# A routed three-layer network in fp32: another bank for layer 3 of odd tiles, and four steps that change places

## The chip, the cores and the metric

The kernel runs on one core of a Trainium2 chip. The metric is the device time of one execution in microseconds (us). Before the change it is 521.77 us, the median of three runs (521.76 to 522.54). All times below are microseconds from the start of the profiled execution's span, unless they are called ns.

## The reference

There are 4096 tokens of 256 numbers and 8 experts. Each expert is a network of three layers (256 to 512, 512 to 512, 512 to 256). A gate picks two experts for each token.

```python
gate = xn @ wg_W + wg_b + (genre_embed @ gg_W + gg_b)     # xn: x, RMS-normalised
gate_w = softmax(gate)
topk_w, topk_i = top_k(gate_w, 2)
cw = sum(one_hot(topk_i, E) * topk_w[..., None], axis=-2)
h1 = relu(einsum('bsh,ehm->bsem', x, W1) + b1)
h2 = relu(einsum('bsem,emn->bsen', h1, W2) + b2)
out_e = einsum('bsen,enh->bseh', h2, W3) + b3
return x + einsum('bseh,bse->bsh', out_e, cw)
```

## The kernel before

The kernel does not run every expert on every token. It computes the gate for all tokens, sorts the (token, expert) pairs by expert, and works through tiles of 128 pairs that belong to one expert. A tile's rows of x are gathered by an indirect DMA, and its results are added to the rows of the output by another. For these inputs there are 67 tiles.

**Banks.** PSUM's eight banks are the tiles PB[0] to PB[7]. Layers 1 and 2 of a tile use PB[0] to PB[3]: layer 1 the first 256 columns of each, layer 2 the others. PB[4] takes transposes of x. PB[5] takes layer 3: its first 256 columns for even tiles, its last 256 for odd ones (L780 to L784). PB[6] takes small things: column totals of the gate's counts in columns 448 to 463 (`totals`, L319 and L320), and the result of one transpose of the gate's values. PB[7] takes the gate's values, and later the index table.

**The front (0 to 29).** x is loaded, transposed on TensorE and multiplied with the gate's weights. The gate of a first part of the tokens (8 of 32 rows per partition, "A") is finished at once, which gives each expert its first tile: tile u of expert u, for u from 0 to 7. Near its end (L473 to L478) come two dummy transposes, `transpose_x(0)` (two transposes on TensorE, and a copy of the result, xT, by ScalarE), and `upright` (a copy of the gate's values from PB[7] to gTs by ScalarE, L218, four small transposes on TensorE, L221, into PB[6]), then a copy of that to graw.

**The head (steps 0 to 6, `head_step`).** Step u works on the first tile of expert u. Meanwhile the routing of all other tokens ("B") goes on, mostly on VectorE. It is a generator, `rest()`, that yields estimates of cost in ns; `more(3200)` draws from it until 3200 are spent or it yields None. Each step calls `more` twice. The seven first calls and the seven second calls draw the same steps wherever they stand. The second call of step 1 holds the totals (TensorE) and some twenty small VectorE operations behind them. Step 2 goes on to the first comparison (L577) of chunk 0 of 4 of the index table. The first call of step 3 holds the rest of chunk 0 (L579, L584) and begins chunk 1, and so on; `table()` issues the table's matmuls (L486) for whatever chunks have been issued. The first call of step 5 holds the gathers of x for tiles 8 to 11, and the second one some POOL operations and the write of the table cwdR.

Every engine executes its own instructions in the order in which this code issues them (`manual_schedule`), and the waits between engines follow from the data. In step u the order of issue is: gather x of tile u+3 (POOL); layer 1 of tile u (TensorE, with its activations on ScalarE, L765); first `more`; transpose of x of tile u+1; layer 3 of tile u-1 (L783); `table()`; layer 2 of tile u (L773, with its activations, L776); second `more`; then for tile u-1 `scaled` (bc = bias times weight, on ScalarE, L749) and `give` (y = layer 3 times weight plus bc, on VectorE, L792, and the scatter-add of y, POOL, L793); last the gather of tile u's weight columns, cg (`gather_cw`, POOL, from the DRAM table cwdA, L645). Tile 0's cg is gathered at the start of step 1. From step 3 on a copy of part of x into the output (SyncE, L842) follows; by the code's dependencies it stands behind the scatters before it.

**The rest (steps 7 and later, `step`).** Steps 8 to 31 work on pairs of tiles of one expert, later steps on single tiles. There x is transposed through DRAM (SyncE: L673 out, L679 back; VectorE: L687), the weights of the step's expert are copied by VectorE (L723, L728, L732, stages 1 to 3), and `scaled` runs on VectorE (L747). The order is: gathers, layer 1 with stage 2, cg of the next step, `scaled` of the step before, stage 1 and xT of the next step, layer 3 and `give` of the step before, stage 3, layer 2.

**The switch.** How many tiles there are is known only at run time. The count is loaded into a register of every engine at step 37, a hint of the branch is given at step 38, and behind step 38 every engine branches to the code for that count (`tc.Switch`), which begins with step 39.

Of the kernel before, what the change touches and what calls it, by code (L numbers as in the profile page):

```python
# [13 lines left out]
ALU = mybir.AluOpType  # L14
# [7 lines left out]
def kernel(  # L22
# [17 lines left out]
    nc = tc.nc  # L40
    V = nc.vector
# [138 lines left out]
    def squares(i, eng):  # L180
        xi = xin[i // TPB][:, i % TPB, :]
        if eng == "A":
            nc.scalar.activation(sqs[eng], xi, AF.Square, accum_out=ss[:, i : i + 1])
        else:
            V.tensor_tensor_reduce(sqs[eng], xi, xi, 1.0, 0.0, ALU.mult, ALU.add, ss[:, i : i + 1])
# [28 lines left out]
    def upright(nq, bank=PB[3], dst=PB[4], copied=False):  # L214

        R = 32 * nq
        if not copied:
            nc.scalar.copy(gTs[0:R, :], bank[0:R, :])  # L218
        gtp = dst[:, 0 : TPB * R].rearrange("p (k r) -> p k r", k=TPB)
        for k in range(TPB):  # L220
            nc.tensor.transpose(gtp[:, k], gTs[0:R, ts(k, P)], ident[0:R, 0:R])  # L221
        return gtp.rearrange("p k (q e) -> p q k e", q=nq)[:, :, :, 0:E]
# [229 lines left out]
    def second_part(some):  # L452

        j0 = GA + 4
        nc.scalar.copy(gTs, PB[3])
        for q in range(2):
            turn_pe(j0 + q, 0, q)
        raw = upright(4, copied=True)
        vps = PB[6][:, 384 : 384 + 2 * E * MC]
        nc.tensor.transpose(vps, vecs, ident[: 2 * E * MC, : 2 * E * MC])  # L460
        for i in range(NA + 10, NI - 4):
            if i == NI - 8:
                V.tensor_copy(vT.rearrange("p l e c -> p (l e c)"), vps)
            squares(i, "V")
        for q in range(2):
            turn_copy(q, "A")
        nc.scalar.copy(graw[:, NA : NA + 4 * TPB, :].rearrange("p (q k) e -> p q k e", q=4), raw)
        for q in range(2):
            turn(j0 + q, 1, 2 + q, "A")
        some(3)  # L470
        for c in range(HC):
            gates(c, (2 * c, 2 * c + 1), PB[7])
        busy(2)  # L473
        for i in range(NI - 4, NI):
            squares(i, "V")
        transpose_x(0)
        raw = upright(2, PB[7], PB[6])
        nc.scalar.copy(graw[:, j0 * TPB : NI, :].rearrange("p (q k) e -> p q k e", q=2), raw)  # L478

    mms = []  # L480
# [181 lines left out]
    def gather_cw(u):  # L662
        for b in tiles(u):
            cg = cgs[b] = ring(run, [P, E], "cg", 6, b)
            fetch(cg, (cwdA if b < E else cwdR)[:, :], b)
# [18 lines left out]
    def transpose_x(u):  # L684
        if u > E:
            for b in tiles(u):
                V.transpose(  # L687
                    xT[:, :, b % 2, :].rearrange("p c (k b) -> p k c b", b=SQ),
                    shs[:, b % 2].rearrange("p k (a c) -> p k c a", a=SQ),
                )  # L690
            return
        bs = tiles(u)
        w = len(bs)
        tp = PB[4][:, 0 : HC * w * BT].rearrange("p (c s t) -> p c s t", c=HC, s=w)
        for k, b in enumerate(bs):
            g = rows(b).rearrange("p (r c) -> p c r", c=HC)
            for c in range(HC):
                nc.tensor.transpose(tp[:, c, k, :], g[:, c], ident)
        nc.scalar.copy(xT[:, :, bs[0] % 2 : bs[0] % 2 + w, :], tp)
# [67 lines left out]
    def layer2(u):  # L767
        _, bb, w2 = ww[u][0:3]
        w = len(tiles(u))
        for n in range(MC):  # L770
# [4 lines left out]
                )  # L775
            nc.scalar.activation(hids[:, 1, n, 0 : w * BT], ph, AF.Relu, bias=bb[:, 1, n : n + 1])  # L776

    def layer3(u):
        w3 = ww[u][3]
        for k, b in enumerate(tiles(u)):  # L780
            po = PB[5][:, ts(b % 2, H)]
            for n in range(MC):
                nc.tensor.matmul(  # L783
                    po, lhsT=hids[:, 1, n, ts(k, BT)], rhs=w3[:, n, :], start=(n == 0), stop=(n == MC - 1)  # L784
                )

    def give(u):

        cws = ww.pop(u)[4]
        for b, (cw, bc) in zip(tiles(u), cws):  # L790
            y = ring(run, [P, H], "y", 2, b)
            V.scalar_tensor_tensor(y, PB[5][:, ts(b % 2, H)], cw, bc, ALU.mult, ALU.add)  # L792
            add = nc.gpsimd.indirect_dma_start(  # L793
                out=orows,
                out_offset=bass.IndirectOffsetOnAxis(ap=index(b), axis=0),
                in_=y,
                in_offset=None,
                bounds_check=NT - 1,
                oob_is_err=False,
                compute_op=ALU.add,  # L800
            )
            if b < E:
                for f in fills[1:]:
                    tc.declare_no_dep(add.ins, f.ins, reason="the first E tiles hold tokens of the first part alone")

            behind = [adds[-1]] if adds else [fills[0]]
            if b == E:
                behind += fills[1:]
            for a in behind:
                tc.add_manual_dep(  # L810
                    add.ins,
                    a.ins.name,
                    mybir.DependencyInfo(mybir.DependencyClass.Sync, mybir.DependencyReason.DATA),
                    reason="a token's row is read and written back",
                )
            adds.append(add)
# [3 lines left out]
    def head_step(u, more):  # L820

        if u + 3 < E:
            gather(u + 3)
        if u == 1:
            gather_cw(0)
        layer1(u)
        more(3200)
        transpose_x(u + 1)
        stage_1(u + 1)
        if u >= 1:  # L830
            layer3(u - 1)
        table()
        layer2(u)
        more(3200)
        if u >= 1:
            scaled(u - 1, "A")
            give(u - 1)
            gather_cw(u)

        if u >= E - 1 - NF:  # L840
            i = NA + (u - (E - 1 - NF)) * (NB // NF)
            fills.append(nc.sync.dma_start(our[:, i : i + NB // NF, :], xr[:, i : i + NB // NF, :]))  # L842
# [8 lines left out]
    def step(u, last, open_end=False):  # L851

        for v in ahead(u, last + 2 * open_end):
            for b in tiles(v):
                gather(b)
        far = E < u + 2 < last + open_end
        if far:
            stow(u + 2)
        if u < last:
            layer1(u)  # L860
            stage_2(u)
        if u + 1 < last:
            gather_cw(u + 1)
        scaled(u - 1)
        if u + 1 < last:
            stage_1(u + 1)
            if u + 1 > E:
                transpose_x(u + 1)
        if far:
            shuffle(u + 2)  # L870
        layer3(u - 1)
        give(u - 1)
        if u + 1 == E:
            transpose_x(u + 1)
        if u < last:
            stage_3(u)
            layer2(u)
# [18 lines left out]
    with tc.manual_schedule():  # L896
        some = first_part()
        for b in range(3):
            gather(b)
        second_part(some)  # L900
        other = rest()

        def routing(ns):
            while ns > 0:
                c = next(other, None)
                if c is None:
                    break
                ns -= c

        routing(100)  # L910
        stage_1(0)
        for u in range(E - 1):
            head_step(u, routing)
        for _ in other:
            pass
        gather_cw(E - 1)
        for u in range(E - 1, CUT):
            if u == CUT - 2:
                _, (nextra,) = nc.values_load_multi_w_load_instructions(
                    nex[0:1, 0:1],  # L920
                    min_val=0,
                    max_val=NREST - NSURE,
                    skip_runtime_bounds_check_because="the tiles behind the first E are NSURE to NREST",
                )
            elif u == CUT - 1:
                tc.switch_hint({e: nextra for e in ENGS}, NREST - NSURE + 1, "tail")
            step(u, SURE, True)
    kept = (ww, ex, cgs)
    state = [{k: list(v) if isinstance(v, list) else v for k, v in d.items()} for d in kept]
    done = list(adds)  # L930
    for k in tc.Switch(nextra, NREST - NSURE + 1, hint="tail"):
        for d, old in zip(kept, state):
            d.clear()
            d.update({b: list(v) if isinstance(v, list) else v for b, v in old.items()})
        adds[:] = done
        with tc.manual_schedule():
            for u in range(CUT, SURE + k + 1):
                step(u, SURE + k)


# [29 lines left out]
```

## Time and profile before

| | |
|---|---|
| median of 3 runs | 521.77 us |
| the profiled execution's own time | 521.67 us |
| its span in the profile | 519.9 us |
| granted TensorE clock, mean | 0.992 |
| instructions | 8677 |
| DMA traffic | 59.25 MB, 114 GB/s in the mean |
| step of a pair (steps 8 to 31), start to start of layer 1 | 13.8 us |
| step of a single tile, start to start of layer 1 | 7.1 us |

The span is what the profile covers; the execution's own time is 1.8 us longer. Engines: PE is TensorE's matmul, PEld its weight load, DVE is VectorE, ACT ScalarE, POOL GpSimd, SP SyncE. A row of the timeline gives start, duration, engine, line, operation, what it writes from what, how many were merged, and in brackets how long the engine was idle before and which work ended that. Ends of matmuls are modelled, so losses are better read from start to start. DMA bandwidth is full from the start to about 58 us: 23 MB are moved between 20 and 100 us, most of it the experts' weights.

### The profile page before, as it was taken

The numbers are of one execution on the slowest core, as the hardware profiler recorded it, in microseconds if no ns is written. First come the engines' busy times: TensorE is split into PE (matmuls) and PEld (weight loads), VectorE is DVE, ScalarE is ACT, GpSimd is POOL, SyncE is SP. The second block draws the span as 40 slices with busy tenths as digits, with TensorE's granted clock in tenths as the row PEclk, the third lists the DMA queues.
The fourth block names the chain that finished last, engine by engine and source line by source line (L and its number), as shares of the span: only waits on it lengthen the run. The fifth ranks groups of instructions, "written<-read, shape, count | busy, mean of one in ns | idle before, by whom it ended". The sixth has DMA issues, their size and how long they took to land. (4 is left out here: it accounts for less than half of the span.)

```text
span 519.9 us, 8677 instructions
## 1 busy us (share of the span) xinstructions
PE 500.8 (96%) x2848; PEld 447.1 (86%) x2848; DVE 226.1 (43%) x549; ACT 169.1 (33%) x415; POOL 286.7 (55%) x241
## 2 busy tenths in 40 slices
PE   8999898999999999999999999999999999999992
PEld 6678898888888888888888888888888889999891
DVE  4776872243443333333344343334433335655450
ACT  4763434222222222222222222222222223443340
POOL 5233466866555556545666655565555455765521
PEclk9999999999999999999999999999999999999996
DMA  8999954743433334334343343333334233433201
GB/s 265 389 412 401 381 133 133 177 106 72 81 69 71 80 67 85 73 82 83 78 83 73 74 80 78 77 79 71 73 71 81 43 82 57 96 68 68 40 4 22
DMA packets 68656, 59.25 MB, mean 114 GB/s; under 512 B 39905, under 2 KB 59570, under 8 KB 68340
## 3 DMA queue, kind: packets, MB, share of 16 engines
q1 hardware_dynamic: 52752, 41.21, 24.5%
q0 software_dynamic: 15136, 17.32, 20.6%
q8 instruction: 24, 0.39, 0.3%
q14 instruction: 36, 0.29, 0.2%
q10 hardware_dynamic: 708, 0.03, 0.1%
HBM read 42.80 MB, written 20.71 MB: 122 GB/s over the span
## 5 line engine op out<-in xcount | busy, mean ns | idle before, releaser
L773 PE MATMUL pb<-hid,big 128*128 128x256 f32 (+1 forms) x1120 | 211.0, 346 | 0.8 <-ACT hid L765 0.8
L773 PEld LDWEIGHTS pb<-hid,big 128*128 128x128 f32 x1120 | 187.0, 191 | 21.6 <-ACT hid L765 1.2
L793 POOL DMA_INDIRECT out_dram<-y,idxR x59 | 100.1, 1697 | 134.5 <-issue 57.5
L776 ACT ACTIVATE hid<-pb,bb 128x256 f32<-128x256 f32 (+1 forms) x140 | 61.7, 441 | 243.8 <-PE pb L773 231.5
L728 DVE COPY big<-w2a 128x2048 f32 x35 | 44.2, 1263 | 151.5 <-PE pb L773 151.5
L762 PE MATMUL pb<-xT,big 128*128 128x256 f32 (+1 forms) x560 | 108.3, 346 | 0.5 <-DVE big L723 0.5
L783 PE MATMUL pb<-big,hid 128*128 128x256 f32 x472 | 107.6, 379 | 0.0
L762 PEld LDWEIGHTS pb<-xT,big 128*128 128x128 f32 x560 | 93.5, 191 | 10.5 <-issue 0.6
L783 PEld LDWEIGHTS pb<-big,hid 128*128 128x128 f32 x472 | 88.8, 190 | 11.6
L645 POOL DMA_INDIRECT big<-in_x_dram,idxR x59 | 76.6, 1298 | 20.6 <-issue 11.9
L645 POOL DMA_INDIRECT cg<-cwdR,idxR x59 | 65.9, 1117 | 18.1 <-issue 18.1
L765 ACT ACTIVATE hid<-pb,bb 128x256 f32<-128x256 f32 (+1 forms) x140 | 60.9, 441 | 43.2 <-PE pb L762 33.4
L792 DVE SCALAR_TENSOR_TENSOR y<-pb,cw,bc 128x256 f32<-128x256 f32 x59 | 26.4, 480 | 59.2 <-PE pb L783 46.7
L723 DVE COPY big<-w1a 128x1024 f32 x35 | 24.3, 695 | 22.4 <-PE pb L762 18.2
L773 PE MATMUL pb<-hid,w2a 128*128 128x128 f32 x256 | 30.3, 276 | 0.1
L773 PEld LDWEIGHTS pb<-hid,w2a 128*128 128x128 f32 x256 | 29.7, 192 | 0.5 <-ACT hid L765 0.3
L793 POOL DMA_INDIRECT out_dram<-y,idxA x8 | 14.6, 1820 | 23.1 <-DVE y L792 22.5
L687 DVE STREAM_TRANSPOSE xT<-gTs 128x256 f32<-128x256 f32 x57 | 22.5, 425 | 5.0 <-DMA gTs<-scr 5.0
L732 DVE COPY big<-w3a 128x1024 f32 x35 | 24.2, 692 | 0.0
L747 DVE TENSOR_SCALAR bc<-b_sb,cw 128x256 f32 x59 | 23.2, 393 | 2.1
L776 ACT ACTIVATE hid<-pb,vT 128x128 f32<-128x128 f32 x32 | 11.8, 368 | 31.0 <-PE pb L773 29.3
L783 PE MATMUL pb<-w3a,hid 128*128 128x256 f32 x64 | 15.4, 384 | 3.3 <-DVE y L792 3.3
(204 smaller groups left out, 251.4 us busy)
## 6 DMA issues: line engine op xcount, KB each, us to landing
w2a<-in_L_cond_W_dram SPq DMA_DIRECT2D x8, 1024.0 KB
scr<-big SPq DMA_DIRECT2D x57, 128.0 KB
gTs<-scr SPq DMA_DIRECT2D x228, 32.0 KB
big<-in_x_dram SPq DMA_DIRECT2D x8, 512.0 KB
w1a<-in_L_cond_W_dram SPq DMA_DIRECT2D x8, 512.0 KB
w3a<-in_L_cond_W_dram SPq DMA_DIRECT2D x8, 512.0 KB
out_dram<-in_x_dram SPq DMA_DIRECT2D x4, 768.0 KB
out_dram<-in_x_dram SPq DMA_DIRECT2D x1, 1024.0 KB
```

The source lines that it names most:

```text
L645: nc.gpsimd.indirect_dma_start(out=dst, out_offset=None, in_=src, in_offset=bass.IndirectOffsetOnAxis(ap=index(b), axis=0), bounds_check=N ...
L723: V.tensor_copy(st1, w1a[:, e].rearrange("p e c m -> p (e c) m"))
L728: V.tensor_copy(st2, w2a[:, ex[u]].rearrange("p e c m -> p (e c) m"))
L732: V.tensor_copy(st3, w3a[:, ex[u]].rearrange("p e c m -> p (e c) m"))
L747: V.tensor_scalar(bc, b3e, cw, None, ALU.mult)
L762: nc.tensor.matmul(ph, lhsT=w1[:, c, ts(m, P)], rhs=cols[:, c, :], start=(c == 0), stop=(c == HC - 1))
L765: nc.scalar.activation(hids[:, 0, m, 0 : w * BT], ph, AF.Relu, bias=bb[:, 0, m : m + 1])
L773: nc.tensor.matmul(ph, lhsT=w2[:, m, ts(n, P)], rhs=hids[:, 0, m, 0 : w * BT], start=(m == 0), stop=(m == MC - 1))
L776: nc.scalar.activation(hids[:, 1, n, 0 : w * BT], ph, AF.Relu, bias=bb[:, 1, n : n + 1])
L783: nc.tensor.matmul(po, lhsT=hids[:, 1, n, ts(k, BT)], rhs=w3[:, n, :], start=(n == 0), stop=(n == MC - 1))
L792: V.scalar_tensor_tensor(y, PB[5][:, ts(b % 2, H)], cw, bc, ALU.mult, ALU.add)
L793: add = nc.gpsimd.indirect_dma_start(out=orows, out_offset=bass.IndirectOffsetOnAxis(ap=index(b), axis=0), in_=y, in_offset=None, bounds_c ...
```

## The change

- The copy from PB[7] to gTs is issued ahead of `transpose_x(0)`, and `upright` no longer makes it.
- Layer 3 writes the first 256 columns of PB[5] for even tiles and of PB[6] for odd tiles (`sums`); `give` reads them there.
- In a head step cg of tile u is gathered at the step's start, right behind the gather of x. Step 0 gathers none, step 1 those of tiles 0 and 1, step 6 those of tiles 6 and 7.
- In a head step `scaled` is issued ahead of layer 3, and the second `more` ahead of layer 2. So the totals, in step 1's second call, follow layer 3 of tile 0 on TensorE, and not layer 2 of tile 1.
- `step` is cut in two: its last part (stage 3 and layer 2) becomes `step_end`. Step 38 runs without it before the switch, and the code behind the switch begins with it. The count is loaded at step 36 and the hint given at step 37.

```diff
@@ second_part @@
+        nc.scalar.copy(gTs[0:64, :], PB[7][0:64, :])
         transpose_x(0)
-        raw = upright(2, PB[7], PB[6])
+        raw = upright(2, PB[7], PB[6], copied=True)
@@ layer3, give @@
+    def sums(b):
+        return PB[5 + b % 2][:, 0:H]
-            po = PB[5][:, ts(b % 2, H)]
+            po = sums(b)
-            V.scalar_tensor_tensor(y, PB[5][:, ts(b % 2, H)], cw, bc, ALU.mult, ALU.add)
+            V.scalar_tensor_tensor(y, sums(b), cw, bc, ALU.mult, ALU.add)
@@ head_step @@
-        if u == 1:
-            gather_cw(0)
+        for k in {0: (), 1: (0, 1), E - 2: (E - 2, E - 1)}.get(u, (u,)):
+            gather_cw(k)
         layer1(u)
         more(3200)
         transpose_x(u + 1)
         stage_1(u + 1)
         if u >= 1:
+            scaled(u - 1, "A")
             layer3(u - 1)
         table()
+        more(3200)
         layer2(u)
-        more(3200)
         if u >= 1:
-            scaled(u - 1, "A")
             give(u - 1)
-            gather_cw(u)
@@ step @@
         if u + 1 == E:
             transpose_x(u + 1)
+
+    def step_end(u, last):
         if u < last:
             stage_3(u)
             layer2(u)
@@ the main loop @@
-        gather_cw(E - 1)
         for u in range(E - 1, CUT):
-            if u == CUT - 2:
+            if u == CUT - 3:
                 _, (nextra,) = nc.values_load_multi_w_load_instructions(
...
-            elif u == CUT - 1:
+            elif u == CUT - 2:
                 tc.switch_hint({e: nextra for e in ENGS}, NREST - NSURE + 1, "tail")
             step(u, SURE, True)
+            if u < CUT - 1:
+                step_end(u, SURE)
@@ behind the switch @@
         with tc.manual_schedule():
+            step_end(CUT - 1, SURE + k)
             for u in range(CUT, SURE + k + 1):
                 step(u, SURE + k)
+                step_end(u, SURE + k)
```

## The prediction

> **What bounds the kernel now.** First the page: is one engine the bound everywhere?
>
> ```profile
> PE 500.8 (96%) x2848; PEld 447.1 (86%) x2848; DVE 226.1 (43%) x549; ACT 169.1 (33%) x415; POOL 286.7 (55%) x241
> ```
>
> TensorE. From 100 to 480 us the table of 10 us windows has 10.00 of 10 for it, so nothing can be won there; what can be won are its gaps. Next, who ended them (us in total, times, longest):
>
> ```profile
> PE pb L783 <- DVE y L792: 3.3, 3, 1.4
> PE pb L221 <- ACT gTs L218: 1.6, 2, 0.9
> PE pb L773 <- ACT hid L765: 0.8, 1, 0.8
> PE pb L486 <- DVE big L584: 0.8, 1, 0.8
> PE pb L762 <- DVE big L723: 0.5, 1, 0.5
> ```
>
> Each is one place of the program. Third, the timelines around the first of them (start, duration). TensorE:
>
> ```profile
> 43.00 2.03 PE L762 MATMUL pb<-xT,w1a 128*128 128x128 f32 x16
> 44.87 0.40 PE L698 MATMUL pb<-ident,xg 128*128 128x128 f32 x2
> 46.30 1.99 PE L783 MATMUL pb<-w3a,hid 128*128 128x256 f32 x8 [1.03 <-DVE y L792]
> ```
>
> and POOL, then ScalarE, before it:
>
> ```profile
> 40.06 0.99 POOL L645 DMA_INDIRECT cg<-cwdA,idxA  x1 [4.28 <-DMA cwdA<-cw8A]
> ```
>
> ```profile
> 42.90 0.37 ACT L776 ACTIVATE hid<-pb,vT 128x128 f32<-128x128 f32 x1 [0.53 <-PE pb L773]
> 45.21 0.51 ACT L749 ACTIVATE bc<-b_sb,cg 128x256 f32<-128x256 f32 x1 [1.95 <-DMA cg<-cwdA,idxA]
> 45.63 1.12 ACT L765 ACTIVATE hid<-pb,vT 128x128 f32<-128x128 f32 x4
> ```
>
> Layer 3 of tile 1 writes one half of PB[5]; it waits for y of tile 0 (DVE, 45.76), which reads the other half: waits go by bank. y waits for bc (ACT L749), bc for cg, the gathered weight columns, and these land only at 45.2, because the gather waited 4.28 us for the table cwdA to be written.
>
> A stall is costed by starts, against the same pair of groups undisturbed (L698 to L783 0.24, L783 to the next 1.72, L762 to L783 1.78, L773 to L762 3.57): 44.87 to 46.30 loses 1.19; 53.48 to 54.79 loses 1.07; 54.79 to 57.62 (the index table waits for DVE) 1.11; 87.29 to 90.63 loses 1.56; 92.93 to 97.13 loses 0.63. Sum 5.56, and some 0.1 more for each restart (46.30 to 48.13 is 1.83, not 1.72).
>
> **The early copy (L218).** Now ACT copies xT at 27.83, after PE's two transposes, then gTs at 28.10 (0.58), and PE waits for it at 28.73. After: gTs first, when the last square ends (27.54), done 28.12, xT done 28.4; PE does its four small transposes from 28.15 and layer 1 from 28.55 instead of 29.12. ACT's table load and layer 2 behind hang on the same chain. **-0.57**; at least -0.3, if PE's gates into PB[7] end later than their modelled 27.15.
>
> **The head (steps 1 to 7).** Four moves at once: bc ahead of layer 2's activations on ACT, the second portion of routing ahead of layer 2, cg a step sooner, two banks. I walk through it in the old times. Each `more(3200)` draws the same steps as before, so DVE's order is unchanged; ACT's, POOL's and PE's change.
>
> Step 1. PE: layer 3 of tile 0 ends 39.06, totals follow (0.36, from 42.64 to 43.00), layer 2 runs 39.42 to 43.0. ACT: free at 38.0, and its next instruction is now bc of tile 0. Its cg is gathered at the same place as before, so it lands at 45.2. Queued behind bc on ACT: layer 2's four activations, which used to run while the gather was in flight. Without wait they run at 0.28 each (four L765 in 1.12): 45.63 to 46.75, the first done at 46.0. Who waits: PE's layer 1 of tile 2 writes PB[0], whose other columns that activation reads. By bank it starts at 46.05 instead of 43.0: **a new wait of 3.05 us**. Bounds: 0 if waits went by columns (the row at 46.30 speaks against it); 5 if cg lands 2 us later.
>
> Then PE runs on: L762 46.05, L783 48.26 (the other bank: no wait for y; the totals in PB[6] were read before y of tile 0), L773 49.98, L762 53.55, L783 55.57, table 57.29. DVE: y of tile 0 stays at 45.76 (totals come 3.6 us sooner to DVE, but the next in its queue is y, which still waits for cg), so its work up to the first comparison of chunk 0 (L577) ends at 53.2 as now; y of tile 1 follows at once (it waited 1.05 for bc), and L584 is done at 56.5, in time for 57.29. So the three waits between 44.87 and 57.62 are gone and the new one stands in their place: the table is at 57.29 against 57.62, only -0.33, and -0.42 with its restart.
>
> Later. DVE stays ahead of chunks 1 to 3 (L584 of chunk 2 at 64.9, needed at 65.5). POOL's order becomes gather, cg, scatter in each step, where cg stood behind the scatter, which waits for y. cg of tile 5 was issued at 87.12 behind POOL's copies and the scatter; now at about 72, so bc and y of tile 5 no longer hold layer 3 of tile 6: -1.56 and a restart. cg of tile 6 was issued at 92.75 and DVE waited 4.55 us for it ahead of L723; now it stands behind the scatter of tile 4 (about 84), issued by 86 and landed by 89 (2.4 us, as 92.75 to 95.13), so L723 is done at 91, needed at 94.4: -0.63 and a restart. Sum at layer 3 of tile 7: 97.87 instead of 100.66: **-2.79**.
>
> Queues that this passes: SP's four copies into the output (L842) each wait for the landing of the scatter before; the last went at 94.73, with the first x rows to be turned (L673, 95.34) behind it. The scatter of tile 5 now has two gathers (2.7 us) ahead of it on POOL, but scatter 4's landing (about 87.3) allows it at 88: the last copy goes at 91.9, xT of the first pair is ready at 104.6 instead of 107.4, layer 1 wants it at 106.5. Hidden, with 1.9 us to spare.
>
> **The clock.** The new wait brings a cost that before never shows: no gap of its is over 1.6 us. The nearest row is the end of the span (columns: window, busy of PE, PEld, DVE, ACT, POOL, then PEclk, DMA share, GB/s):
>
> ```profile
> 510.00:520.00 10.00, 0.00 (x0) 0.00 (x0) 0.31 (x1) 0.00 (x0) 1.55 (x1) 0.59 0.11 14
> ```
>
> PEclk 0.59 over the 9.87 us up to the span's end is 1.8 us at full and the rest at half: the clock was halved at 511.8, 2.0 us after the last matmul's end (507.90 + 1.89). [...] By the row, 2 us of idle can be enough; the gap is 1 us longer. I take the row. [...]
>
> **The pairs (8 to 31).** y of an even tile waited for the odd tile's matmuls too (DVE y from L783, 46.7 us in 29 waits); now it starts some 1.7 us sooner. PE is full there and waits for no y: 0.
>
> **The switch.** Now:
>
> ```profile
> 482.44 1.14 ACT L765 ACTIVATE hid<-pb,bb 128x128 f32<-128x128 f32 x4 [3.48 <-PE pb L783]
> 482.86 3.94 PE L773 MATMUL pb<-hid,big 128*128 128x128 f32 x32 [0.85 <-ACT hid L765]
> ```
>
> ACT takes its branch after the last activation of layer 2 and needs 3.48 us to its next instruction; PE loses 1.01 (480.12 to 482.86 against 1.73 a tile before) and 0.1 restart. After: ACT branches after layer 1's activations (473.7) and is back at 477.1; layer 2's first activation was due at 475.85, but it catches up (0.28 each against PE's 0.89) before PE needs PB[0] at 478.33. DVE's stage_3 copy (0.68) comes behind the branch, at about 478.2 to 478.9, needed at 480.1. But PE: its queue held 3.57 us of layer 2 ahead of the branch; now it holds what is left of layer 1 and 1.73 us of layer 3. The branch records (line 965) have PE's at 476.6 and its first instruction behind at 478.0, 1.4 us; DVE's 475.3 to 478.2 and POOL's 475.7 to 478.6, 2.9 us each. PE gets to the branch at about 472.2; layer 2 wants to load at 474.55. With 1.4 us nothing is lost, with 3.4 about 1.1. I take the 2.9 of the two engines whose branch no long queue stood before: 0.85 lost instead of 1.1. **-0.25**, between -1.1 and +0.3. The load of the count and the hint, a step sooner, cost PE no gap now (its 462.2 record lies in full windows): 0.
>
> **Sum.** Against the profiled execution's own 521.67 (span 519.9): -0.57 - 2.79 + 1.55 - 0.25 = -2.06, 519.61; the median of the runs is 0.10 above it, so **519.7**.
>
> **Rivals.**
> 1. The clock stays up over the gap: 518.2. [...] Against: the last row. 0.24.
> 2. No new wait: bc's cg lands a us or two sooner, or layer 1 doesn't wait for the activation of its bank. Then DVE's L584 (56.5) sets the table: 0.8 below rival 1, 517.4. For: the gather's 4.1 us from 41.05 are in full DMA traffic and could be shorter. Against: cwdA's write took 6.3 us in it. 0.14.
> 3. Slower: one place, ACT's queue at step 1. Each us that cg of tile 0 lands later is a us of PE, since its layer 2 activations are now behind it (before, it was y alone). [...] 0.12.
> 4. It gives back what it takes (cg late by a us, or PE's branch at its full 3.4): 520.8 to 522.8. 0.12.
> The likeliest case, the wait with the clock halved, is left with 0.38.
>
> **How the numbers follow.** A measurement of this kernel tells about 0.2% (1.04 us) from no change. Below 520.7 lie my case, rivals 1 and 2: 0.76; within 0.2% 0.12; slower 0.12. Range: from rival 2 (517.4) to 521.9, which leaves out rival 3 and the outermost of the others.
>
> **What would show it.** ACT L749 of tile 0 still at about 44.6, with 6 us or more idle before it, released by the DMA of cg; PE L762 of tile 2 released by ACT L776, 3 us; PEclk below 1 in the window 40:50; no PE wait for y in the head; L221's wait about 0.6 shorter; at 470 to 475 PE idle before L773 with no releaser but its own branch, and ACT's 3.48 no longer followed by a PE gap. I am wrong if L749's wait does not put L776 behind it, if L762 doesn't wait for it, or if PE waits anew between 97 and 470 us.

## The result, and the profile after

The changed kernel takes 519.27 us in the median of five executions (517.64 to 519.69), beside 521.77 (521.70 to 522.54) for the kernel before: a ratio of 0.9944, with a 95% interval of 0.9927 to 0.9961. 519.7 was predicted. The profiled execution is the fastest of the five, 517.64 with a span of 515.9; the experiments look for the reason.

The waits of TensorE after the change (us in total, times, longest):

```profile
PE pb L763 <- ACT hid L777: 3.4, 2, 2.7
```

The row of the early copy (L221) has shrunk from 1.6 to 0.7. No row for y is left, and none for the index table. In their place stands layer 1 (now L763), waiting for layer 2's activations (L777) of the tile before. The timeline of TensorE shows where (start, duration, ..., idle before and what ended it):

```profile
38.54 3.82 PE L774 MATMUL pb<-hid,w2a 128*128 128x128 f32 x32
45.10 2.05 PE L763 MATMUL pb<-xT,w1a 128*128 128x128 f32 x16 [2.75 <-ACT hid L777]
...
56.28 1.13 PE L487 MATMUL pb<-big 128*128 128x69 f16 x16
```

ScalarE behind it:

```profile
44.29 0.51 ACT L750 ACTIVATE bc<-b_sb,cg 128x256 f32<-128x256 f32 x1 [7.18 <-DMA cg<-cwdA,idxA]
```

bc of tile 0 stands in ScalarE's queue with 7.18 us of idleness before it, because its weight column lands only then (POOL issued the gather at 39.04, after 4.16 us of waiting for cwdA). The four activations behind it run from 44.70 on without a pause, and TensorE, which was free at 42.11 (38.54 + 3.57), starts at 45.10. That is a loss of 2.99, where two waits for y and one for the table were before.

A second wait is new. In step 6:

```profile
80.79 0.71 PE L763 MATMUL pb<-xT,w1a 128*128 128x128 f32 x4 [0.66 <-ACT hid L777]
```

On ScalarE two of the four activations that it waits for come late. In an undisturbed tile the second, third and fourth follow each other at 0.89:

```profile
77.10 0.37 ACT L777 ACTIVATE hid<-pb,vT 128x128 f32<-128x128 f32 x1 [0.59 <-PE pb L774]
78.90 0.37 ACT L777 ACTIVATE hid<-pb,vT 128x128 f32<-128x128 f32 x1 [1.44 <-PE pb L774]
80.37 0.37 ACT L777 ACTIVATE hid<-pb,vT 128x128 f32<-128x128 f32 x1 [1.10 <-PE pb L763]
```

And the switch, before:

```profile
480.12 1.89 PE L783 MATMUL pb<-big,hid 128*128 128x256 f32 x8
...
486.64 1.95 PE L762 MATMUL pb<-xT,big 128*128 128x128 f32 x16
```

and after:

```profile
470.25 1.89 PE L788 MATMUL pb<-big,hid 128*128 128x256 f32 x8
471.98 3.73 PE L774 MATMUL pb<-hid,big 128*128 128x128 f32 x32
475.56 1.95 PE L763 MATMUL pb<-xT,big 128*128 128x128 f32 x16
```

Layer 2 starts 1.73 us after layer 3, as in an undisturbed tile, and from layer 3 to the next layer 1 it is 5.31 instead of 6.52: the branch costs TensorE nothing now. ScalarE comes back late, at 473.55 after 2.67 us of idleness, runs two activations back to back and has caught up.

### The profile page after: what moved, and what is told of

It reads as the page before. It is cut to its first block, busy times and chain, and to the rows that moved or that the text cites. A ratio compares the mean times of both kernels' runs of the same rounds, so it can differ in the third digit from the quotient of the medians.

```text
span 515.9 us, 8677 instructions
## 1 busy us (share of the span) xinstructions
PE 499.8 (97%) x2848; PEld 446.7 (87%) x2848; DVE 229.6 (45%) x549; ACT 170.4 (33%) x415; POOL 290.5 (56%) x241
## 5 line engine op out<-in xcount | busy, mean ns | idle before, releaser
L798 POOL DMA_INDIRECT out_dram<-y,idxR x59 | 96.9, 1642 | 127.4 <-issue 56.8
L777 ACT ACTIVATE hid<-pb,bb 128x256 f32<-128x256 f32 (+1 forms) x140 | 61.6, 440 | 245.5 <-PE pb L774 242.7
L763 PE MATMUL pb<-xT,big 128*128 128x256 f32 (+1 forms) x560 | 108.2, 346 | 0.0
L763 PEld LDWEIGHTS pb<-xT,big 128*128 128x128 f32 x560 | 93.5, 191 | 9.9
L646 POOL DMA_INDIRECT big<-in_x_dram,idxR x59 | 81.9, 1389 | 23.2 <-issue 15.6
L646 POOL DMA_INDIRECT cg<-cwdR,idxR x59 | 68.2, 1156 | 18.0 <-issue 18.0
L797 DVE SCALAR_TENSOR_TENSOR y<-pb,cw,bc 128x256 f32<-128x256 f32 x59 | 28.5, 483 | 47.3 <-issue 24.3
L733 DVE COPY big<-w3a 128x1024 f32 x35 | 25.3, 722 | 0.5 <-issue 0.5
L777 ACT ACTIVATE hid<-pb,vT 128x128 f32<-128x128 f32 x32 | 11.4, 366 | 24.6 <-PE pb L774 23.0
L763 PE MATMUL pb<-xT,w1a 128*128 128x128 f32 x128 | 16.1, 277 | 3.4 <-ACT hid L777 3.4
```

Source lines behind the costliest of these rows:

```text
L646: nc.gpsimd.indirect_dma_start(out=dst, out_offset=None, in_=src, in_offset=bass.IndirectOffsetOnAxis(ap=index(b), axis=0), bounds_check=N ...
L733: V.tensor_copy(st3, w3a[:, ex[u]].rearrange("p e c m -> p (e c) m"))
L763: nc.tensor.matmul(ph, lhsT=w1[:, c, ts(m, P)], rhs=cols[:, c, :], start=(c == 0), stop=(c == HC - 1))
L797: V.scalar_tensor_tensor(y, sums(b), cw, bc, ALU.mult, ALU.add)
L798: add = nc.gpsimd.indirect_dma_start(out=orows, out_offset=bass.IndirectOffsetOnAxis(ap=index(b), axis=0), in_=y, in_offset=None, bounds_c ...
```

## The experiments

Theory A is the prediction's: the new wait stands behind bc of tile 0, it costs 3 us by itself, and in most executions a stretch of halved TensorE clock behind it takes more. Its rival B: nothing happens to the clock, and the executions differ because the weight column lands at different times. Each part of the change also has a share of its own to be found.

One measure separates the head from everything else: **head**, from the start of layer 1 of tile 0 to the start of layer 3 of tile 7 in the profiled execution. It is 71.54 in the kernel before:

```profile
29.12 2.05 PE L762 MATMUL pb<-xT,w1a 128*128 128x128 f32 x16
...
100.66 1.89 PE L783 MATMUL pb<-w3a,hid 128*128 128x256 f32 x8
```

and 69.57 after:

```profile
28.31 2.05 PE L763 MATMUL pb<-xT,w1a 128*128 128x128 f32 x16
...
97.88 1.89 PE L788 MATMUL pb<-w3a,hid 128*128 128x256 f32 x8
```

The column "halved" lists the stretches in which the profile's record of TensorE's clock shows half speed, before the end of the work.

| kernel | median, us | ratio to before (95%) | head | halved |
|---|---|---|---|---|
| after, again | 519.51 | 0.9949 (0.9936 to 0.9962) | 69.66 | none |
| gap filled | 518.45 | 0.9927 (0.9915 to 0.9940) | 70.31 | none |
| bc of tile 0 late | 518.61 | 0.9926 (0.9914 to 0.9938) | 70.81 | 55.95 to 59.37 |
| the same, table late | 515.82 | 0.9871 (0.9856 to 0.9886) | 68.04 | none |
| copy only | 521.29 | 0.9979 (0.9963 to 0.9995) | 71.39 | none |
| switch only | 521.12 | 0.9964 (0.9948 to 0.9981) | 72.71 | 29.82 to 33.23 |
| one bank | 518.52 | 0.9908 (0.9879 to 0.9936) | 70.46 | 45.26 to 48.67 |
| no output copies | 518.25 | 0.9911 (0.9880 to 0.9942) | 71.76 | 45.20 to 52.02 |
| weight columns only | 518.73 | 0.9931 (0.9914 to 0.9947) | 68.07 | none |
| banks only | 524.97 | 1.0052 (1.0035 to 1.0068) | 74.46 | 58.33 to 61.74, 99.29 to 102.70 |
| bc back | 517.40 | 0.9902 (0.9886 to 0.9919) | 67.85 | none |
| bc back, table late | 514.52 | 0.9851 (0.9834 to 0.9867) | 65.96 | none |

The kernel before had a median of 522.19 beside the first four, 522.70 beside the next four and 522.40 beside the last four; the ratios are to these. No run has the changed kernel and one of the last eight side by side, so these are compared with it by their ratios.

**The changed kernel again.** No edit.

> The changed kernel unaltered, to see how its times are spread and what goes with them. Its five times so far are 517.6 once (the profiled one: a wait of 3.0 us at layer 1 of tile 2, granted clock full) and 519.2 to 519.7 four times. Theory A (the clock is halved behind the 3 us of idle in most executions, and stays up in some, depending on where the gap lies): two groups again, near 517.6 and near 519.3, the upper ones with a mean granted clock some 0.003 lower (3.4 us at half of 516); if the profile falls into the upper group, PEclk is below 1 between 40 and 60 us. Theory B (the gather of tile 0's weight columns lands 1.5 to 2 us later in the upper group): the same times, but with full clock, and an activation of bc that starts near 46.

518.32, 518.69, 519.51, 519.58 and 519.76. The profiled one is 518.32, with the wait at 45.84 (2.84 long) and the clock never halved; the upper three have a mean clock of 0.989 to 0.990, the lower two of 0.995 and 0.992. So the spread repeats, and it goes with the clock.

How far does a mean clock tell of a halved stretch in an execution without a profile? Behind the end of the work the clock is at half speed for 4.9 to 8.1 us in the fourteen profiles, which by itself gives a mean of 0.995 to 0.992; one stretch of 3.41 us at half speed takes 0.003 more (half of 3.41, of a span of 516). So (an estimate from these spans) 0.991 or less means a halved stretch, 0.993 or more means none, and 0.992 leaves it open. By that measure the kernel before isn't free of such stretches either: none of its 11 executions beside the first four kernels shows 0.991 or less, but 15 of 22 beside the next four do and 6 of 7 beside the last four. Its one profile shows none; "switch only" below shows a place. The ratios hold a part of this, so where it matters the executions at 0.993 or more are compared by themselves.

**The gap filled.** Behind layer 2 of tile 1, 24 transposes of the identity that nobody reads.

```diff
         layer2(u)
+        if u == 1:
+            busy(24)
```

> 24 dummy transposes (about 2.7 us) on TensorE behind layer 2 of tile 1, in the gap before layer 1 of tile 2, and nothing else. Theory A (clock): the gap shrinks to 0.3 us, the clock stays up in every execution, all times near 517.6 and no upper group; median 1.6 below the changed kernel's. Theory B (late landing): the dummies change nothing of what the gap waits for; median as the changed kernel's, 519.3, with the same spread.

```profile
42.25 2.78 PE L227 MATMUL pb<-ident 128*128 128x128 f32 x24
45.37 2.05 PE L763 MATMUL pb<-xT,w1a 128*128 128x128 f32 x16 [0.34 <-ACT hid L777]
```

Layer 1 starts at 45.37, within the 45.10 to 45.84 of the two profiles without the filler, so no useful work moves; yet the median falls by 1.06 (1.6 was expected), and all five executions lie between 517.88 and 518.63, with mean clocks of 0.992 to 0.995. The upper group is gone. B gives no reason for that; A does.

**bc of tile 0 late.** `scaled(0)` goes back behind layer 2, in step 1 alone.

```diff
-            scaled(u - 1, "A")
+            if u > 1:
+                scaled(u - 1, "A")
...
         layer2(u)
+        if u == 1:
+            scaled(u - 1, "A")
```

> The changed kernel, but in step 1 alone bc of tile 0 stands behind layer 2's activations again. Theory A: no wait of layer 1 of tile 2 for an activation; the next limit is VectorE, whose index table chunk 0 is ready at 55.5, so TensorE waits there about 2.3 us: 0.8 us sooner than the changed kernel at full clock, 516.8, and 518.4 in those executions in which the new gap of 2.3 us halves the clock. Rival: bc of tile 0 so late costs again what it cost before the change (1.2 us at layer 3 of tile 1), 518 or more at full clock.

```profile
55.85 1.16 PE L487 MATMUL pb<-big 128*128 128x69 f16 x16 [2.37 <-DVE big L585]
56.81 5.03 PE L774 MATMUL pb<-hid,w2a 128*128 128x128 f32 x32
```

The wait at 45 is gone, and another of nearly its size has come up: TensorE reaches the table sooner, and VectorE's chunk 0 (L585) is not ready. Layer 2 behind it takes 5.03 instead of 3.82: the clock record has half speed from 55.95 to 59.37. In the 3.41 us before that, TensorE was idle for 2.37.

**The same, and the table late.** The table's matmuls are also left out of steps 3 and 4, so that those of chunks 0 to 2 come a step later, and chunk 3's with them.

```diff
-        table()
+        if u not in (3, 4):
+            table()
```

> As the one before, and the matmuls of the index table are issued later: none behind layer 3 in steps 3 and 4, chunk 0 inside the first routing call of step 4, chunks 1 to 3 in the first one of step 5. If the gap at step 1 and the table's wait for VectorE are all that is left in the head, TensorE runs through and is 3.3 us sooner at step 5: 514.3 with full clock in every execution. Rival: what is won is lost again at the first pair, whose x rows come through SyncE's queue behind the copies into the output: 516 to 517, with layer 1 of tile 10 waiting for VectorE's transposes.

515.82: 2.8 less than without it. 514.3 was to be had if the wait of step 6 had stayed away; it is still there, and longer (layer 1's last four matmuls at 79.39, 1.68 us behind L777).

**The early copy only**, in the kernel before.

```diff
+        nc.scalar.copy(gTs[0:64, :], PB[7][0:64, :])
         transpose_x(0)
-        raw = upright(2, PB[7], PB[6])
+        raw = upright(2, PB[7], PB[6], copied=True)
```

> The kernel before with the early copy to gTs alone. By the prediction 0.57 us sooner, by what the changed kernel's trace shows at the start of layer 1 of tile 0 (28.31 instead of 29.12) 0.8. Both theories of the head leave the rest as before: the wait for y at layer 3 of tile 1 stays, because the weight columns land as much sooner as the rest. 0.6 to 0.8 below the kernel before. Rival: the start is sooner but the head is held by DMA (the weight columns of tile 0), then 0 to 0.3.

A ratio of 0.9979, some 1.1 us, with an interval that reaches from 0.3 to 1.9. Among the executions with a mean clock of 0.993 or more it is 1.2 (medians of 520.65 and 521.84). In its profile layer 1 of tile 0 starts at 28.06, against 28.97 in the profile of the next kernel, whose front is without the copy and equally early (L227 at 25.67 and 25.69).

**The switch only**, in the kernel before: `step` cut in two, count and hint a step sooner, nothing else of the change.

```diff
+    def step_end(u, last):
         if u < last:
             stage_3(u)
             layer2(u)
...
             step(u, SURE, True)
+            if u < CUT - 1:
+                step_end(u, SURE)
```

> The kernel before with the switch ahead of layer 2 alone. By the prediction's sum 0.25 sooner (TensorE waits 0.85 for its own branch); by the changed kernel's trace (TensorE's first instruction 0.4 us behind its branch record, no gap) 1.1 sooner.

0.9964, some 1.9 us (1.0 to 2.7); among the executions with a mean clock of 0.993 or more it is 1.1 (medians of 520.77 and 521.84). Layer 3 starts at 474.05 and layer 2 at 475.78, 1.73 again: no gap. TensorE's branch record stands at 473.27 and its first record behind it at 473.66, 0.4 us. The kernel shows something else by chance: its front, the same as before's, ran into half speed in the profiled execution. Two windows cut at the clock record's own edges (length, then busy time of PE, PEld, DVE, ACT, POOL, then PEclk, DMA share, GB/s):

```profile
26.40:29.82 3.42, 1.75 (x13) 1.49 (x14) 1.30 (x8) 1.57 (x5) 1.00 (x1) 1.00 1.02 418
29.82:33.23 3.41, 3.41 (x18) 3.41 (x18) 2.66 (x11) 2.75 (x8) 1.20 (x4) 0.50 1.03 403
```

Two waits of about 1 us, for the first rows of x and for gTs, fall into one window, the first for the most part: 1.67 idle in the sum, and the next window is halved. So it is not the single gap that counts.

**One bank.** The changed kernel, with layer 3 of all tiles in the two halves of PB[5] as before.

```diff
     def sums(b):
-        return PB[5 + b % 2][:, 0:H]
+        return PB[5][:, ts(b % 2, H)]
```

> The changed kernel with layer 3 of all tiles in the two halves of one bank again. Theory A: in the changed kernel y is done before the next tile's layer 3 starts at every step of the head (44.8 against 47.2, 52.2 against 54.5, 60.5 against 62.9, 83.6 against 88.7), so the second bank is worth nothing: times as the changed kernel's, two groups near 518.3 and 519.5 on this chip, and no wait of layer 3 for y. Rival: the bank takes away waits of its own; then layer 3 waits for y in the head and the kernel is 0.5 us or more slower than the changed one.

Beside the other moves the second bank is worth nothing that can be seen (0.9908, its interval reaching from 0.9879 to 0.9936, against 0.9949 and 0.9944 with it): no wait for y comes back in its profile, since the wait ahead of it at 45 lets y of tile 0 finish. Its executions are spread more widely than was expected, from 515.61 to 519.88; the lowest has a mean clock of 0.989, and nothing on record explains it. And here the profiled execution caught the halved clock that the changed kernel's own profile had missed:

```profile
45.18 3.68 PE L763 MATMUL pb<-xT,w1a 128*128 128x128 f32 x16 [3.00 <-ACT hid L777]
```

```profile
41.84:45.25 3.41, 0.41 (x5) 0.23 (x3) 0.34 (x1) 0.88 (x3) 0.00 (x0) 1.00 1.06 403
45.25:48.67 3.42, 3.42 (x16) 3.42 (x17) 3.21 (x9) 1.75 (x6) 2.69 (x2) 0.50 1.07 406
```

The transposes behind layer 1 start at 48.70, 3.52 after it instead of 1.89: half speed costs 1.63 once. The same gap in the changed kernel's profile lay across an edge:

```profile
40.22:43.63 3.41, 2.14 (x20) 1.95 (x18) 1.10 (x10) 0.00 (x0) 1.00 (x1) 1.00 1.07 405
43.63:47.04 3.41, 1.94 (x17) 1.94 (x18) 2.08 (x5) 2.51 (x8) 1.45 (x1) 1.00 1.04 403
```

1.27 and 1.47 of idle in two windows, and no loss of clock. By this account the profiled execution is the fastest because an edge split its gap.

**No output copies.** The changed kernel without SyncE's four copies of x into the output in the head, so that three quarters of the output's rows lack x. They were tried as a cause of the wait in step 6.

```diff
-        if u >= E - 1 - NF:
+        if u < 0:
```

> The changed kernel without SyncE's four copies of x into the output in steps 3 to 6; so three quarters of the output rows lack x, and its time counts for the head alone. In every trace of a changed head the last activations of layer 2 in step 5 come 1 to 2.5 us late and cost TensorE 0.7 to 1.7 us in layer 1 of step 6, while such a copy is under way. Theory C (the copies' traffic delays what ScalarE waits for, its instructions' fetch for one): that wait is gone, 0.8 us sooner than the changed kernel at equal clock. Rival: it stays, and has nothing to do with the copies.

Inconclusive. The wait in step 6 is absent, but it is absent with one bank too, where the copies are in place. What the time shows is the clock, halved for two windows in the profiled execution (45.20 to 52.02).

**Weight columns only**, in the kernel before: cg a step sooner, ahead of layer 1.

```diff
-        if u == 1:
-            gather_cw(0)
+        for k in {0: (), 1: (0, 1), E - 2: (E - 2, E - 1)}.get(u, (u,)):
+            gather_cw(k)
```

> The kernel before with the weight columns gathered a step sooner, and nothing else. If this move alone makes the head's gain: y of tile 1 no longer waits for bc, so chunk 0 of the table is ready 1.1 sooner, and the waits before layer 3 of tile 6 (1.56) and layer 1 of the first pair (0.63) are gone; the 1.2 at layer 3 of tile 1 stays. 3.4 below the kernel before at equal clock, and no gap over 1.3 us that could halve the clock. By the prediction's attribution (the moves win together): 2.4. Rival: bc behind layer 2 on ScalarE is what holds y, then less than 1.

518.73, 3.7 less than before, in one move out of five. Two of its four executions have mean clocks of 0.990, so full clock in all of them, as expected, did not come. Two waits are left of the head's old five, and each stands in a window of its own:

```profile
46.46 1.99 PE L783 MATMUL pb<-w3a,hid 128*128 128x256 f32 x8 [1.04 <-DVE y L792]
...
56.63 1.14 PE L486 MATMUL pb<-big 128*128 128x69 f16 x16 [0.82 <-DVE big L584]
```

**Banks only**, in the kernel before: odd tiles in PB[6].

> The kernel before with the second bank for layer 3, and nothing else. All waits of layer 3 for y go (3.8 us of loss by the starts), but what y waits for stays: TensorE then waits some 3.3 us for chunk 0 of the table (VectorE, 57.6 as before), and for the copy of the first pair's weights. 0 at equal clock; 1.5 slower where the longer gap halves the clock. Rival: the waits that go are won: 2 to 4 faster.

524.97: slower, by 0.52%. TensorE's wait for y of tile 0 is gone, so it arrives at the table sooner; but VectorE's chunk 0 is no sooner there.

```profile
57.80 1.16 PE L486 MATMUL pb<-big 128*128 128x69 f16 x16 [2.73 <-DVE big L584]
...
98.66 1.86 PE L762 MATMUL pb<-xT,big 128*128 128x256 f32 x5 [2.05 <-DVE big L723]
```

The waits are not shortened but merged into two long ones, and both are followed by a window at half speed. All four executions have mean clocks of 0.986 to 0.987. In the profile before, TensorE's waits for y (1.03, 0.91 and 1.39 us) had been splitting the idle time into portions with no half speed behind them.

**bc back.** The changed kernel with `scaled` and the second `more` behind layer 2 again in all head steps.

```diff
         if u >= 1:
-            scaled(u - 1, "A")
             layer3(u - 1)
         table()
-        more(3200)
         layer2(u)
+        more(3200)
         if u >= 1:
+            scaled(u - 1, "A")
             give(u - 1)
```

> The changed kernel with bc and the second routing call behind layer 2 again, in all head steps. No activation stands behind bc, so the 3 us at layer 1 of tile 2 go; chunk 0 of the table is ready at the same time (the weight columns of tile 0 set it), so TensorE waits 2.4 us there. 0.8 below the changed kernel at equal clock; 1.2 more where the gap of 2.4 halves the clock. Rival: y comes later and layer 1 of the first pair or layer 3 waits: no gain over the changed kernel.

517.40, or 0.9902 against the changed kernel's 0.9944 and 0.9949: of its moves these two together cost some 2 us. No run separates them. In its profile the head is 67.85, neither the wait at 45 nor that of step 6 is there, and the table waits in place of them (55.60, 1.66 us), cut in two by a window's edge (0.85 and 0.81 idle by the records); its other three executions, at 517.35 to 517.46, have a lower mean clock (0.991 to 0.992 against 0.995), as if the gap had fallen into one window there; no profile shows it.

**bc back, and the table late**, as in the fourth kernel.

> As the one before, with the table's matmuls issued later (none behind layer 3 in steps 3 and 4). No gap over 1.3 us is left in the head behind the first tile, so full clock in every execution and 3 us or more below the changed kernel, 6.5 below the kernel before. Rival: the next limit (SyncE's queue to the first pair) takes half of it back.

```profile
PE pb L699 <- DMA xg<-in_x_dram,idxA: 1.3, 1, 1.3
...
PE pb L788 <- DVE offs L527: 0.2, 1, 0.2
```

514.52, the best of all: 7.9 us below the kernel before and, by ratios whose intervals lie apart, nearly 1% below the changed one. Of its waits only the last lies in the head; the others are in the front. One execution, 515.37, has a mean clock of 0.990, which by the measure above still means a halved stretch; full clock in all of them was expected.

## Why the prediction was right, and where it was not

**The early copy: right.** The last square on ScalarE, before and after:

```profile
27.35 0.19 ACT L183 ACTIVATION_READ_ACCUMULATOR sqA<-big 128x1 f32 x1
```

```profile
27.14 0.19 ACT L183 ACTIVATION_READ_ACCUMULATOR sqA<-big 128x1 f32 x1
```

From its end to layer 1 it is 1.58 us before (27.54 to 29.12) and 0.98 after (27.33 to 28.31): 0.60, against 0.57. The whole shift of layer 1's start is 0.81; the other 0.21 is in the front ahead of it, whose last matmuls (L227) start at anything from 25.67 to 27.51 in the fourteen profiles.

**The new wait: right in place, cause and size.** It was put at 43.0 to 46.05 with ScalarE's bc in front of the activations; it is at 42.11 to 45.10, 2.99 instead of 3.05, with the releasers that were named. The table's wait was to shrink to nearly nothing and it vanished: 56.28 to 57.24 is the undisturbed 0.96. "Bc back" is its counter-proof: with the activations in front again the wait is not there, though cg lands no sooner (bc runs at 44.36).

**The rest of the head: right but for one term.** All waits for y and for L723 went, as said. The head gained 1.97, not 2.79. The missing 0.82 is the wait in step 6 (0.93 lost: layer 1 takes 2.72 from 78.62 to the transposes at 81.34, and 1.79 undisturbed), which no step of the prediction has: there I let ScalarE's activations follow TensorE at once. In the changed kernel's profile two of them in step 5 come about 0.9 and 1.5 us later than TensorE's pace. What delays them stays open. The wait appears in five of the seven profiles in which bc stands ahead of layer 2 in step 5, and in none of the seven in which it doesn't; taking the output copies away didn't decide it. ScalarE's own instructions may have come late, which that experiment's expectation named. In four of the five profiles the last late activation starts 0.14 to 0.24 us after a packet of 8192 bytes on an instruction queue of the DMA (q14) has landed; in the fifth it starts 0.12 us before. Such a packet comes at that place in the other profiles too, so this doesn't settle it.

**The clock: right in direction and size for most executions.** The sum has +1.55 for a halved clock behind one gap of 3.05 us; no run shows that term, which was an estimate of the author's. What the runs show in its place is a loss of 1.63 where a profile has it ("one bank"), and executions above 519 that lie 1.6 to 2.1 us over the profiled one; one stretch of 3.41 us at half speed can cost 1.71 at the most, so not all of the 2.1 is that. Three of these four have mean clocks of 0.989 to 0.990; the fourth, 519.33, has 0.992, which leaves it open. And half speed was not behind every such gap: it followed 3.00 us of idle that lay in one window ("one bank"), and not the 1.27 and 1.47 into which an edge split the gap in the changed kernel's profile. The step was also wrong to say that this cost "before never shows": the mean clocks of the kernel before tell of it in 21 of the 40 executions beside the experiments. In the profiled execution rival 1 came true: 518.2 was its number, 517.64 the time, and the clock stayed up over the gap (1.00 in both windows). The row that the prediction went by, half speed after some 2 us of idle at the end of the work, held inside the work too: waits of 3.00, 2.73, 2.37 and 2.05 us were each followed by half speed, in stretches of 3.41 us.

**The switch: mis-sized.** Predicted -0.25, measured -1.2 (6.52 to 5.31): the gap of 1.01 and its restart are gone. The failing term is TensorE's branch, "I take the 2.9 of the two engines whose branch no long queue stood before". TensorE's own row, 1.4 us, was the nearer one, and even it is too long: the branch record is at 469.48 and the next at 469.87, 0.4 us. The term's sum is off as well: from the branch at 472.2, 2.9 us lead to 475.1, which is 0.55 behind the 474.55 wanted and not 0.85, so by its own figures it was -0.55. ScalarE (2.7) and POOL (3.0) do take about what was assumed, and VectorE took 0.6; none holds TensorE.

**The pairs: right.** No wait of TensorE lies between 97 and 470 us. x of the first pair is transposed at 104.77 and wanted at 106.52, close to the predicted 104.6 and 106.5.

**The sum.** By the profiles: copy 0.60, front 0.21, head 1.97, switch 1.2, together the 4.0 between the two spans; then 1.6 back from the profiled execution to the median. The prediction had 3.6 and 1.55. Two misses of opposite sign (0.82 too hopeful in the head, 0.95 too cautious at the switch) nearly cancel, so the median's 0.4 from the forecast is partly luck. The larger miss is one of bookkeeping: the head's gain was told as that of four moves together. By the experiments it is the gain of one, the earlier weight columns (a head of 68.07 with them alone); the bank alone is a loss and beside the others nothing that can be seen, and bc and the routing call ahead of layer 2 cost some 2 us together.

## What to carry to other kernels

Before an operation is put earlier in an in-order queue, look at what it waits for: here a bias term that waited 7 us for a transfer was put in front of activations that TensorE needed. Removing one wait moves the engine to the next one; when what the next one waits for is fixed in time, the waits merge, and a merged wait can cost the clock as well (here 2.73 and 2.05 us, each with 3.41 us at half speed behind it). In these profiles it was the idle time in one window of 3.41 us that told, and not the single gap (two waits of about 1 us, 1.67 in one window, were followed by half speed; one wait of 2.75, split into 1.27 and 1.47, was not), so price idle time that way. A change of several parts is worth taking apart: here one part brought all of the head's gain, and two others spent some of it.

## What the runs showed of the chip

**Half speed in TensorE's clock record.** In all fourteen profiles the record of half speed starts at a multiple of 3.413 us from the first record of full speed (before: 6.69 to 511.86, 148.00 times 3.413; after: 6.08 to 507.84, 147.00 times), and in the middle of the work it lasts 3.413 us (once 6.827, 45.20 to 52.02 in "no output copies"). Counting TensorE's idle time in each such window (ends of matmuls are modelled), windows at full speed with 2.05 ("banks only"), 2.32 ("no output copies"), 2.37 ("bc of tile 0 late"), 2.73 ("banks only") and 3.00 us ("one bank") of idle were each followed by half speed (as were seven at the end of the work, with 2.05 to 3.02), and those with up to 1.51 never. In between the picture isn't clean: 1.67 ("switch only") was followed by it, 1.79 and 1.81 (both "after, again") were not. What decides between 1.51 and 2.05 stays open. A window already at half speed is another case: in the one stretch of 6.827 ("no output copies") TensorE was idle for only 0.63 us of the first window, and the second was at half speed all the same.

**The front's waits are interchangeable.** When TensorE's front ends early (L227 at 25.67 to 26.31 instead of 27.08), it waits 0.7 to 1.3 us for the first gathered rows of x instead, and layer 1 starts within 28.06 to 29.41 in all profiles.

**Branches.** With the branch issued ahead of layer 2, TensorE was through it in 0.4 us and VectorE in 0.6, where before they took 1.4 and 2.9; ScalarE, POOL and SyncE still took 2.7 to 3.2. The hint was also given a step sooner, and no run here separates the two.
